# The feed-forward part's hidden values: bias from ScalarE to VectorE, rounding from GpSimd to ScalarE

## The chip, the cores and the metric

The kernel runs on one core of a Trainium2 chip. The metric is the device time of one execution in microseconds. The core's engines that matter here: TensorE (PE, matrix products; its weight loads are listed as PEld), VectorE (DVE), ScalarE (ACT), GpSimd (POOL) and SyncE (SP), whose queue issues the DMAs. Each takes its own instructions in the order in which the program gives them; they wait for one another by semaphores.

## The reference

The input is 32 images of 56 x 56 pixels with 96 channels. Layer 0 is a convolution block with weights mixed per image: 1x1 expansion to 384 channels, 3x3 depthwise convolution, 1x1 projection, each with batch normalization, and the input added. Layer 1 treats the 3136 pixels of an image as tokens: a layer normalization, a token mixer that goes through a Fourier transform and back, an addition, and then the feed-forward part that the change concerns:

```
t = t + _L1_ffn_ref(_ln_t(t), W1, b1, W2, b2)

q_mul = lambda x: _float_quantize(x, 5, 2)     # 8 bits: 5 of exponent, 2 of mantissa
q_acc = lambda x: _float_quantize(x, 5, 10)    # 16 bits: float16

def _qlinear(x, W, b):
    y = q_acc(jnp.einsum('bsk,nk->bsn', q_mul(x), q_mul(W)))
    return q_acc(y + q_mul(b))
h = jax.nn.relu(_qlinear(x, W1, b1))           # 96 -> 384
y = _qlinear(h, W2, b2)                        # 384 -> 96; rounds h to 8 bits first
```

So a hidden value is a sum rounded to float16, plus a bias, rounded to float16 again, cut at zero, and rounded to 8 bits before the second product.

## The kernel before

Images are independent, and the kernel keeps several of them in flight: the convolution of one runs beside the Fourier and feed-forward steps of earlier ones. `record(b)` (line 767) lists the operations of image b. An image has two halves h for the convolution, 3 chunks c of 128 hidden channels for each, and 4 strips `st` of 784 pixels (`T`) for the token steps.

- Convolution. `by_tensor` (line 928) computes a chunk with PE, with DMAs that regroup the pixels before it (hp<-h) and after it (h<-hp). `by_vector` (line 869) computes a chunk with VectorE: PE expands, ScalarE moves the values to SBUF and makes a first pass over each half of the tile (ACT h<-h,small), VectorE adds the eight other taps (DVE h<-h,small,h 128x784, in place), ScalarE cuts at zero.
- Token mixer. Layer-norm moments (`ln`) with bn_stats on VectorE and the root on GpSimd, products `ha` and `g`, then seven groups of frequencies (`za`, `zb`, `tmpa`, `tmpb`, `zo`, `y`), in which ScalarE and VectorE alternate, then the way back.
- Feed-forward part (the loop `for st in range(NS)`), once a strip: the mixer's result is added (`xs`), moments and normalization (`nt`, 8 bits), a turn back on PE (`n8`), and then for each of the 3 chunks of hidden channels, from line 1412 on:
  - PE: two products of 392 columns into two banks of PSUM (`up`);
  - ScalarE: a copy from PSUM to `h16`, float16;
  - ScalarE: in place, bias and Relu (from line 1429);
  - GpSimd: a copy that rounds `h16` to `h8`, 8 bits (from line 1434);
  - later PE: the second product (`down`), which reads the three `h8` tiles.
  That is 12 such tiles an image and 384 in all. `h16` has 2 buffers, `h8` has 6 (lines 735 and 736). After `down`, ScalarE copies to `y16`, VectorE adds a bias to it in float16 (DVE TENSOR_SCALAR y<-y,fb 96x784, the only operation of this kind in the image loop), GpSimd adds it to `xs`, and a DMA writes the result.

What runs in which order is written by a planner. `Plan.add` (line 219 on) takes for each operation an engine, an assumed duration, a due time and the buffers that it reads and writes. To each due time a number out of a fixed list is added by the operation's place in the list. `Plan.order` (line 269) simulates the engines with the assumed durations and returns the operations in the order of their simulated starts; `for op in plan.order(): op.emit()` (line 1478) issues them. `Pinned` (line 370) keeps each engine's instructions in that order. The planner only names the engine of an operation; which engine executes it is decided by the function that is passed to be emitted. So two operations that the planner starts one after the other reach the program one after the other, whichever engine they go to. All pinned instructions bear line 380, which is why the profile tells them apart by tile names and shapes.

The helper that gives each engine's instructions its waits works from the tiles: an instruction waits for the last one that wrote what it reads, and for the last ones that read what it overwrites.

Of the kernel before, what the change touches and what calls it, by code (L numbers as in the profile page):

```python
# [14 lines left out]
AF = mybir.ActivationFunctionType  # L15
ALU = mybir.AluOpType
# [202 lines left out]
class Plan:  # L219
# [16 lines left out]
    def add(self, eng, dur, due, emit, reads=(), writes=(), takes=(), size=0, port=None, slack=0.0):  # L236
        op = Op()
        op.seq = len(self.ops)
        due += NUDGE[op.seq % len(NUDGE)]
        if eng in ("DVE", "ACT") and any(isinstance(k[0], Buf) and isinstance(k[0].ring, Banks) for k in reads):  # L240
            due -= HURRY
        op.eng, op.dur, op.due, op.emit = eng, dur, round(due, 3), emit
        op.takes, op.size, op.slack = list(takes), size, slack
        op.port = eng == "POOL" if port is None else port
        op.after, op.ready, op.end = [], 0.0, None
        before = set()
        for key in reads:
            if key in self.writer:
                before.add(self.writer[key])
        for key in writes:  # L250
            if key in self.writer:
                before.add(self.writer[key])
            before.update(self.readers.get(key, ()))
        for key in writes:
            self.writer[key] = op
            self.readers[key] = []
        for key in reads:
            if key not in writes:
                self.readers.setdefault(key, []).append(op)
        op.left = len(before)  # L260
        for b in sorted(before, key=lambda o: o.seq):
            b.after.append(op)
        op.bufs = list(dict.fromkeys(key[0] for key in (*reads, *writes) if isinstance(key[0], Buf)))
        for b in op.bufs:
            b.users += 1
        self.ops.append(op)
        return op
# [118 lines left out]
def kernel(  # L386
# [26 lines left out]
    def const(shape, dt, name):  # L413
        return cp.tile(shape, dt, tag=name, name=name)
# [62 lines left out]
    fb1 = const([128, NC3], F32, "fb1")  # L477
# [261 lines left out]
    for r in (r_in, r_xs, r_da, r_dd, r_g2, r_yt):  # L739
# [6 lines left out]
    te, ve, se, po, sy = (  # L746
        Pinned(tc, e) for e in (nc.tensor, nc.vector, nc.scalar, nc.gpsimd, nc.sync)
    )
# [3 lines left out]
    def cols(engine, n):  # L752
        return {"DVE": n / 960 + 0.125, "ACT": n / 1200 + 0.05}[engine]

    def halves(ap):
        return ap.rearrange("p (j t) -> p j t", j=2)
# [10 lines left out]
    def record(b):  # L767
# [572 lines left out]
        for st in range(NS):  # L1340
# [56 lines left out]
            def turn_back(ps=ps, nt=nt):  # L1397
                for q in range(SQ):
# [9 lines left out]
                    saturate=False,  # L1408
                ),
                reads=[(ps, 0)], writes=[(n8, 0)],  # L1410
            )
            h8s = []
            for c in range(NC3):
                ps, h16, h8 = Buf(banks, 2), Buf(r_h16), Buf(r_h8)

                def up(c=c, ps=ps, n8=n8):
                    for j in range(2):
                        te.matmul(
                            ps.pair[:, 512 * j : 512 * j + TH], fw1[:, 128 * c : 128 * c + 128],
                            n8.ap[:, j * TH : j * TH + TH], start=True, stop=True,  # L1420
                        )

                add("PE", 0.36, due + 7, up, reads=[(n8, 0)], writes=[(ps, 0)], takes=[ps, h16])
                add(
                    "ACT", cols("ACT", T), due + 8,
                    lambda ps=ps, h16=h16: se.copy(halves(h16.ap), halves(ps.pair)[:, :, 0:TH]),
                    reads=[(ps, 0)], writes=[(h16, 0)],
                )
                add(
                    "ACT", 0.86, due + 9,  # L1430
                    lambda c=c, h16=h16: se.activation(h16.ap, h16.ap, AF.Relu, bias=fb1[:, c : c + 1]),
                    writes=[(h16, 0)],
                )
                add(
                    "POOL", 0.82, due + 9.5,
                    lambda h16=h16, h8=h8: po.tensor_copy(h8.ap, h16.ap, saturate=False),
                    reads=[(h16, 0)], writes=[(h8, 0)], takes=[h8],
                )
                h8s.append(h8)
# [35 lines left out]
    for b in range(NB):  # L1475
        record(b)
# [115 lines left out]
```

## Time and profile before

| what | value |
|---|---|
| three timed runs | 4315.35, 4319.36, 4329.76 us (median 4319.36) |
| profiled execution, time | 4307.71 us |
| profiled execution, span from first to last instruction | 4305.9 us |
| granted TensorE clock, mean | 0.967 |
| VectorE, busy | 3661.1 us, 9036 instructions |
| ScalarE, busy | 3092.0 us, 6281 instructions |
| GpSimd, busy | 1627.6 us, 1332 instructions |
| copy to h16 on ScalarE (ACT CAST h<-ps 128x784) | x384, mean 815 ns |
| ScalarE, rounding of the normalized values (ACT n<-ps 96x784 fp8e5) | x128, mean 827 ns |
| ScalarE, Relu without bias (ACT h<-h 128x784 f32) | x192, mean 858 ns |
| taps on VectorE (DVE h<-h,small,h 128x784) | x1536, mean 1063 ns |

How to read it: a group's line gives the engine, the operation, the tile written and those read, the shapes, the number of such instructions, then their busy time in us and the mean of one in ns, and after the bar the idle time of the engine just before them with what ended it. A timeline's line gives start, duration, and the instruction; "x3" merges three in a row, and consecutive instructions of VectorE and ScalarE overlap a little in it, so that durations add up to slightly more than the time from start to start. The chain of waits goes back from the last instruction, at each step to what released it, and gives shares of the span.

In the middle of the run the same pattern of instructions returns with every image: the period of the h tiles is 126.6 us from 1360.0 to 1486.6 and 126.0 us from 1486.6 to 1612.6.

### The profile page before, as it was taken

What the parts mean: (1) busy time and instruction counts of PE and PEld (TensorE: products, weight loads), DVE (VectorE), ACT (ScalarE), POOL (GpSimd) and SP (SyncE); (2) the same over time, 40 slices, a digit from 0 to 9 for tenths busy, and PEclk for the clock granted to TensorE, in tenths of its full rate; (3) what the DMA queues carried; (4) which work ended last, traced back from release to release, by engine and by line L of the source; (5) the groups of instructions that cost most, each with busy time, mean ns of one, the idle gap of its engine ahead of it and who ended that gap; (6) DMA issues with size and microseconds to landing.
All of it is one profiled execution on the core that took longest, in us unless ns stands there. A gap on an engine that the chain in (4) does not pass through costs nothing.

```text
span 4305.9 us, 104378 instructions
## 1 busy us (share of the span) xinstructions
PE 3833.1 (89%) x40066; PEld 2422.4 (56%) x40066; DVE 3661.1 (85%) x9036; ACT 3092.0 (72%) x6281; POOL 1627.6 (38%) x1332
## 2 busy tenths in 40 slices
PE   2899999899999998899999999998999999999985
PEld 0466565555565555555556556555565555556564
DVE  5898988888998888988898898887988888998762
ACT  1467777677787776777777787776777777787665
POOL 1224333443333443433443434343433443434333
PEclk9999999999999999999999999999999999999995
DMA  4776667676667766667677667766667776667651
GB/s 118 142 166 150 158 170 173 148 170 158 154 172 180 170 162 157 152 154 174 155 175 169 151 159 175 175 158 152 151 155 178 163 171 159 153 160 171 148 143 58
DMA packets 427749, 679.25 MB, mean 158 GB/s; under 512 B 155062, under 2 KB 290678, under 8 KB 427206
## 3 DMA queue, kind: packets, MB, share of 16 engines
q1 hardware_dynamic: 421632, 668.08, 66.3%
q8 instruction: 316, 5.18, 0.6%
q10 hardware_dynamic: 5618, 4.49, 0.4%
q14 instruction: 183, 1.50, 0.1%
HBM read 300.21 MB, written 211.04 MB: 119 GB/s over the span
## 4 chain that ended last, share of the span: by engine, by line
DVE 36%; PE 28%; ACT 22%; issue 6%; DMA 5%; POOL 1%; SPq 0%; POOLq 0%; ACTq 0%; DVEq 0%
PE ps L380 28%; DVE h L380 8%; ACT h L380 8%; DVE ln L380 6%; ACT nt L380 4%; DVE ha L380 3%; DVE za L380 3%; DVE tmpa L380 3%; DVE tmpb L380 3%; DMA hp<-h 3%; DVE zb L380 3%; DVE wk L380 2%; ACT tmpa L380 2%; ACT g L380 1%; DVE wkc L380 1%
## 5 line engine op out<-in xcount | busy, mean ns | idle before, releaser
L380 DVE SCALAR_TENSOR_TENSOR h<-h,small,h 128x784 f32<-128x784 f32 x1536 | 1569.5, 1063 | 61.0 <-ACT h L380 54.8
L380 POOL CAST h<-h 128x784 fp8e5<-128x784 f16 x384 | 604.2, 1578 | 1397.9 <-ACT h L380 1397.8
L380 PE MATMUL ps<-x,wk 97*32 97x435 f32 (+2 forms) x3840 | 686.7, 569 | 21.0 <-DVE wk L380 17.3
L380 PE MATMUL ps<-dftb_s,g 112*64 112x112 f32 (+1 forms) x3776 | 420.3, 281 | 31.4 <-DVE ln L380 16.6
L380 ACT ACTIVATE h<-ps 128x435 f32<-128x435 f32 (+2 forms) x768 | 389.7, 546 | 67.9 <-PE ps L380 66.8
L380 DVE SCALAR_TENSOR_TENSOR ha<-ps,ln,nshift 120x192 f32<-120x192 f32 x896 | 306.0, 407 | 154.7 <-PE ps L380 153.7
L380 POOL TENSOR_TENSOR ln<-ln,mhalf 120x7 f32<-120x7 f32 (+1 forms) x256 | 429.2, 1676 | 21.3
L380 PE MATMUL ps<-hp,wg 32*32 32x392 f32 x12288 | 390.0, 523 | 27.8 <-issue 20.9
L380 PEld LDWEIGHTS ps<-dftb_s,g 112*64 112x64 f32 (+1 forms) x3776 | 341.0, 168 | 128.6 <-issue 40.9
L380 DVE BATCH_NORM_STATS2 ln<-ps 112x6 f32<-112x96 f32 (+1 forms) x1792 | 318.1, 248 | 86.5 <-PE ps L380 83.1
L380 PEld LDWEIGHTS ps<-x,wk 97*32 97x32 f32 (+1 forms) x3840 | 206.9, 125 | 297.1 <-issue 191.1
L380 ACT ACTIVATE hp<-ps,small 128x392 f32<-128x392 f32 x384 | 212.3, 591 | 225.0 <-PE ps L380 183.3
L380 ACT ACTIVATE h<-h,fb 128x784 f16<-128x784 f16 x384 | 366.4, 965 | 0.3
L380 ACT ACTIVATE nt<-ps,ln 112x96 fp8e5<-112x96 f32 x896 | 302.5, 437 | 75.0 <-DVE ln L380 74.9
L380 ACT ACTIVATE h<-h 128x784 f32<-128x784 f32 x192 | 164.4, 858 | 264.5 <-DVE h L380 264.5
L380 PE MATMUL ps<-w1c,x 96*120 96x192 f32 x1792 | 340.1, 337 | 6.6 <-issue 6.6
L380 POOL TENSOR_TENSOR xs<-xs,y 96x784 f32<-96x784 f32 x128 | 237.2, 1854 | 251.5 <-DVE y L380 164.4
L380 PEld LDWEIGHTS <-fw 96*128 96x128 fp8e5 (+1 forms) x1536 | 155.1, 114 | 284.8 <-issue 209.6
L380 PEld LDWEIGHTS ps<-w1c,x 96*120 96x120 f32 x1792 | 296.9, 188 | 32.7 <-issue 28.3
L380 ACT CAST h<-ps 128x784 f16<-128x784 f32 x384 | 302.5, 815 | 17.5 <-PE ps L380 16.1
L380 PEld LDWEIGHTS ps<-hp,wg 32*32 32x32 f32 x12288 | 221.4, 106 | 166.5 <-issue 83.3
L380 PE MATMUL ps<-h,wkc 128*96 128x392 f32 x768 | 284.9, 519 | 0.0
(171 smaller groups left out, 7180.0 us busy)
## 6 DMA issues: line engine op xcount, KB each, us to landing
hp<-h SPq DMA_DIRECT2D x384, 217.5 KB
h<-hp SPq DMA_DIRECT2D x384, 196.0 KB
gd<-g SPq DMA_DIRECT2D x384, 192.0 KB
g<-gd SPq DMA_DIRECT2D x192, 336.0 KB
dd<-ddd SPq DMA_DIRECT2D x128, 392.0 KB
yt<-yd SPq DMA_DIRECT2D x128, 336.0 KB
xd<-park SPq DMA_DIRECT2D x128, 294.0 KB
xs<-xd SPq DMA_DIRECT2D x128, 294.0 KB
```

The costliest lines, as they stand in the source:

```text
L380: return self.tc.keep_in_program_order(method(*args, **kwargs))
```

## The change

The bias and the Relu of h go to VectorE: one tensor_scalar with two operations, addition of the per-partition bias and maximum with zero, float16 in place. The rounding to 8 bits goes from GpSimd to ScalarE, as an activation Copy. The engine names, durations and due times that are handed to the planner stay as they were ("ACT" and "POOL"), so that the simulated schedule and the order in which all operations are issued are the same: VectorE meets a bias at the place in the order where ScalarE had it, and ScalarE meets a rounding where GpSimd had it.

```diff
                 add(
                     "ACT", 0.86, due + 9,
-                    lambda c=c, h16=h16: se.activation(h16.ap, h16.ap, AF.Relu, bias=fb1[:, c : c + 1]),
+                    lambda c=c, h16=h16: ve.tensor_scalar(
+                        h16.ap, h16.ap, fb1[:, c : c + 1], 0.0, ALU.add, ALU.max
+                    ),
                     writes=[(h16, 0)],
                 )
                 add(
                     "POOL", 0.82, due + 9.5,
-                    lambda h16=h16, h8=h8: po.tensor_copy(h8.ap, h16.ap, saturate=False),
+                    lambda h16=h16, h8=h8: se.activation(h8.ap, h16.ap, AF.Copy, saturate=False),
                     reads=[(h16, 0)], writes=[(h8, 0)], takes=[h8],
                 )
```

## Prediction

> **What bounds the kernel now.** I read the busy times first, then the chain of work that ended last, then one image's time on each engine (1486.6 to 1612.6 us), then the groups of the three operations concerned.
>
> ```profile
> PE 3833.1 (89%) x40066; PEld 2422.4 (56%) x40066; DVE 3661.1 (85%) x9036; ACT 3092.0 (72%) x6281; POOL 1627.6 (38%) x1332
> ```
>
> ```profile
> DVE 36%; PE 28%; ACT 22%; issue 6%; DMA 5%; POOL 1%; SPq 0%; POOLq 0%; ACTq 0%; DVEq 0%
> ```
>
> Three engines share the chain, so an average says little. The timeline of VectorE over one image sorts it out (columns: start us, us, then the instruction; the last bracket is idle time before it).
>
> ```profile
> 1497.56 0.91 DVE L380 SCALAR_TENSOR_TENSOR tmpb<-zb,tmpb 128x112 f32<-128x112 f32 x1
> ...
> 1520.66 2.38 DVE L380 SCALAR_TENSOR_TENSOR wk<-wpw_s,mix,wk 97x384 f32<-97x384 f32 x3
> 1522.96 0.26 DVE L380 SCALAR_TENSOR_TENSOR zb<-tmpb,zb 128x112 f32<-128x112 f32 x1
> 1523.15 0.90 DVE L380 TENSOR_TENSOR ln<-ln 120x7 f32<-120x7 f32 x2
> ...
> 1543.43 14.85 DVE L380 SCALAR_TENSOR_TENSOR h<-h,small,h 128x784 f32<-128x784 f32 x15
> ...
> 1562.43 1.25 DVE L380 BATCH_NORM_STATS2 ln<-ps 120x6 f32<-120x96 f32 x7 [1.97 <-PE ps L380]
> ```
>
> From 1579.4 to the next image's 1543.5 (about 90 us of 126) VectorE idles 2.1 us in all: this phase is its own. From 1546.4 to 1577.7 PE runs with two short gaps and VectorE waits for it: PE's phase. GpSimd at the same moments:
>
> ```profile
> 1497.31 1.03 POOL L380 CAST h<-h 128x784 fp8e5<-128x784 f16 x1 [7.35 <-ACT h L380]
> ...
> 1521.58 1.05 POOL L380 CAST h<-h 128x784 fp8e5<-128x784 f16 x1 [10.88 <-ACT h L380]
> 1522.80 1.15 POOL L380 CAST h<-h 128x784 fp8e5<-128x784 f16 x1 [0.17 <-ACT h L380]
> ```
>
> The tmpb operation that takes 0.91 us under the first cast takes 0.27 at 1502.23, with no cast; the two ln operations that take 0.90 under the third take 0.24 at 1500.29. So a cast stops VectorE. ScalarE around the last two casts:
>
> ```profile
> 1520.55 0.97 ACT L380 ACTIVATE h<-h,fb 128x784 f16<-128x784 f16 x1
> 1521.40 0.48 ACT L380 COPY zo<-ps 112x384 f32<-112x384 f32 x1
> 1521.76 0.97 ACT L380 ACTIVATE h<-h,fb 128x784 f16<-128x784 f16 x1
> 1522.61 0.60 ACT L380 ACTIVATE tmpa<-ps,fa 128x280 f32<-128x280 f32 x1
> ```
>
> And the groups (busy us, mean ns of one, idle before):
>
> ```profile
> L380 POOL CAST h<-h 128x784 fp8e5<-128x784 f16 x384 | 604.2, 1578 | 1397.9 <-ACT h L380 1397.8
> ...
> L380 ACT ACTIVATE h<-h,fb 128x784 f16<-128x784 f16 x384 | 366.4, 965 | 0.3
> ...
> L380 DVE TENSOR_SCALAR y<-y,fb 96x784 f16<-96x784 f16 x128 | 54.4, 425 | 52.5 <-ACT y L380 49.7
> ```
>
> **What the Trainium skill says.** "SBUF — State Buffer", section "Who interferes with whom": GpSimd and a VectorE operation with two SBUF inputs, or in a two-port mode, exclude each other; the loser blocks for the whole instruction. The trace agrees (0.91 against 0.27 us above). "VectorE: DVE Perf Modes", section "The perf-mode tier table": tensor_scalar on 16-bit SBUF data reaches the fourfold mode; the y row, same length and form, has 402 ns at least and 411 in the median. "ScalarE: Activation LUTs", section "What ACT_TABLE_LOAD costs": an ACTIVATE with immediates is 186 ns + 0.833 ns an element, and a pointer operand adds some 93 ns: estimates 839 and 932 ns for 784 elements; the trace has 858 (the Relu without bias) and 965.
>
> **The change, part by part.** An image has 12 h tiles (384 in all). Starts are counted, since neighbours overlap by about 0.08 us.
>
> *Removed from ScalarE:* 12 bias+Relu, 0.85 us each start to start (1520.55 to 1521.40). *Added there:* 12 roundings. No row has f16 to fp8 on ScalarE; between the n row (fp8 from PSUM, 827 ns) and the 858 Relu I take 0.83, start to start 0.75. Its own sum is a gain of 1.2 us an image, in 72% busy, so worth nothing by itself.
>
> *Added on VectorE:* 12 tensor_scalar, 0.33 us start to start, as y's (1505.17 to 1505.50). That form has one operation and this one two; bounds 0.33 and, at half the rate, 0.33+784/4/960 = 0.53. I take 0.33, since y shows the mode and the rest is alike. It is 3.96 us an image.
>
> *Removed from GpSimd:* 12 casts. GpSimd does not bound, but what they blocked comes back to VectorE. Start to start against the same operations unblocked: tmpa pair 1486.68 (1.25 for 0.60) 0.65; za pair 0.64; tmpb 0.65; wk 2.30 for 1.92, 0.38; ln pair 0.66; ln triple at 1594.40 (0.90 for 0.25) 0.65. Sum 3.63 us, plus some 0.4 on taps. Over all VectorE rows that overlap a cast, time above the unblocked median is 130 us, or 4.06 an image. So 3.96 in, 4.06 out: balanced. Behind the casts GpSimd has the park copy, the wg products and the layer-norm root. They start up to 1 us earlier; each still meets one VectorE operation, so I put that at zero, with 0.3 us an image either way as its bound. No DMA and nothing on SP's queue moves.
>
> *The new waits.* VectorE's bias waits for ScalarE's copy: in the steady images the copy ended 0.2 to 3 us before VectorE comes to that turn, so it stops nobody. ScalarE's rounding waits for VectorE, and behind it queue the evictions of PSUM. By the turns of the changed program, nine of an image's twelve fall in VectorE's phase; I walk them with the running shift of VectorE:
> - 0 to 2 (1588 to 1595): +0.99-0.65 = +0.34. ScalarE stands some 0.5, 0.6 and 1.1 us for the biases, and its first pass over the next tap tile ends at 1597.7 instead of 1595.8. The tap that needs it comes at 1597.47+0.34: just in time, and ScalarE's wait of 1.80 us at 1597.58 is the cover. If 0.1 us of cover is gone, VectorE pays.
> - 3 and 4 (1485.9 to 1489): +0.66-1.29, shift -0.29. The second rounding fills a gap of 0.99 before zo.
> - 5 (1496.8): +0.33-0.65, shift -0.61.
> - 6 and 7: wk ends at 1521.97, bias until 1522.38, rounding, then tmpa at 1523.19 and until 1523.79. VectorE is at its za (1524.30 before) at 1523.31, and waits 0.50. Shift -0.61-0.38+0.66-0.66+0.50 = -0.49.
> - 8: +0.33: shift -0.16 where the image hands over to PE.
> - 9 to 11 lie in PE's phase: +0.66 against 1.4 us between VectorE's last x update (1560.46) and the PE transposes that read it (1561.90). Covered.
>
> So 31 images x -0.16 = -5 us. In the tail (after 4150) VectorE idles and the chain runs through copies, Relus and casts: a tile's bias costs 0.41+0.06 in place of 0.97, saving about 0.5 us on some 14 tiles, -7; against it one bias waits from 4244.9 to 4250.3 and holds the residual addition (4247.89) behind it for 2.8 us. Tail -4. Total -9 against the profiled execution (span 4305.9, time 4307.7, 12 below the median of 4319.4). The forecast is put on the median: 4310.
>
> **Rivals.**
> - *The hand-over costs (slower).* The place is ScalarE in turns 0 to 2 and 6: it stands for a bias that VectorE does late, and evictions behind it come 0.9 to 1.9 us late. For: two of my steps have margins near 0.1 us. Against: ScalarE idles 28%. It decides once ScalarE's lateness at a tap tile's first pass is over 0.1 us; if 1.3 of the 1.9 us passes on, 31 x 1.3 = 40 in place of the -5: with the tail's -4, 4355.
> - *The freed port pays in full (faster).* If turn 6 doesn't wait, and the taps' 0.4 counts: -0.16-0.50-0.4 = -1.06 an image, -33, with the tail 4282. For: the chain view has 85 of the 130 blocked us on it, and only 204 of the 384 bias places (67 us). Against: the wk operations precede bias 6 in every image.
> - *The bias runs at half rate:* 9 x 0.20 x 31 = 56 on top of the forecast, 4366. Against: y.
> - That the change isn't made is excluded: the changed program has 384 more instructions on VectorE, 384 fewer on GpSimd, and as many as before on ScalarE.
>
> **How the numbers follow.** About 0.3% (13 us) is what a measurement of this kernel can tell from no change: 4306.4 to 4332.3. Balance 50%, its own range 4294 to 4330 (0.4 us an image either way, and the tail's gain): of that 17 faster, 29 same, 4 slower. Hand-over 27%, slower. Freed port 19%, faster. Half rate 4%, slower. So faster 0.36, same 0.29, slower 0.35. The range, 4280 to 4354, leaves out the half rate, the dearer part of the hand-over and the better end of the freed port, some 2 in 10.
>
> **What would show it.** VectorE's new row at 0.41 us x384 and its busy time within 20 us of 3661; ScalarE's rounding near 0.83; the tmpb, za and ln groups at their unblocked means; ScalarE's waits for VectorE up by some 4 us an image, and VectorE's for tmpa by 0.5. I am wrong if the bias row is over 0.45 us, if other GpSimd work takes the casts' place in blocking VectorE, or if VectorE waits for ScalarE at the taps.

## The result and the profile after

| kernel | median of the runs | ratio to before, 95% interval |
|---|---|---|
| before, 7 runs | 4319.36 us | |
| changed, 7 runs (4343.98 to 4371.79) | 4350.05 us | 1.008 (1.0056 to 1.0103) |

The change makes the kernel 31 us slower, where 9 us less were forecast; 4350 is near the upper end of the stated range (4280 to 4354), on the other side of before. The profiled execution took 4343.98 us, span 4342.2 (before 4305.9), mean granted TensorE clock 0.961 (before 0.967). Busy times and the chain that ended last, from the page of the changed kernel:

```profile
PE 3858.6 (89%) x40066; PEld 2508.2 (58%) x40066; DVE 3670.9 (85%) x9420; ACT 3085.8 (71%) x6281; POOL 1059.9 (24%) x948
```

```profile
PE 37%; DVE 30%; ACT 23%; issue 4%; DMA 3%; POOL 0%; SPq 0%; DVEq 0%; POOLq 0%; ACTq 0%
```

VectorE has 384 instructions more and is busy only 9.8 us longer: the balance of added biases and freed port came out. But its share of the chain fell from 36 to 30% and PE's rose from 28 to 37%. The two new groups (busy us, mean ns of one, idle before):

```profile
L380 ACT ACTIVATE h<-h 128x784 fp8e5<-128x784 f16 x384 | 328.4, 856 | 160.3 <-DVE h L380 157.0
L380 DVE TENSOR_SCALAR h<-h,fb 128x784 f16<-128x784 f16 x384 | 158.2, 419 | 28.0 <-ACT h L380 28.0
```

Both durations are near the forecast's (0.83 and 0.41). New is what stands before the rounding: ScalarE idles 157 us for VectorE's biases. The list of waits says the same (waiting engine and tile, then whom for; us in total, times, longest):

```profile
ACT h L380 <- DVE h L380: 362.1, 338, 4.2
...
PE ps L380 <- ACT y L380: 92.4, 57, 2.2
...
DVE za L380 <- ACT za L380: 73.5, 59, 2.2
```

Before, these were 264.5, 45.1 and 21.2 us. All three meet in turns 6 to 8 of the hidden tiles: in the 29 images counted below, 76 of the 160 us that ScalarE idles before roundings lie there, 60 of the 92 of PE, and 23 of the 74 of VectorE (43 of these lie in turns 3 to 5). The timeline of the changed kernel there (start, us, instruction; idle before in brackets):

```profile
1153.61 0.75 DVE L380 TENSOR_SCALAR h<-h,fb 128x784 f16<-128x784 f16 x2
...
1154.06 0.86 ACT L380 ACTIVATE h<-h 128x784 fp8e5<-128x784 f16 x1 [1.66 <-DVE h L380]
...
1155.90 0.51 DVE L380 SCALAR_TENSOR_TENSOR za<-ps,fa,tmpa 128x280 f32<-128x280 f32 x1 [0.86 <-ACT za L380]
...
1156.84 0.85 ACT L380 ACTIVATE h<-h 128x784 fp8e5<-128x784 f16 x1
...
1158.02 0.48 ACT L380 COPY y<-ps 112x384 f32<-112x384 f32 x1
1158.04 2.30 POOL L380 TENSOR_TENSOR wg<-mask,small 128x512 f32<-128x512 f32 x2 [1.12 <-DVE small L380]
...
1158.55 0.49 PE L380 MATMUL ps<-n,fw 96*128 96x392 fp8e5 x2 [2.24 <-ACT y L380]
...
1159.33 1.83 DVE L380 SCALAR_TENSOR_TENSOR h<-h,small,h 128x784 f32<-128x784 f32 x1
```

and the same matmuls, the tap, the wg products and rounding 8 before:

```profile
1148.56 0.49 PE L380 MATMUL ps<-n,fw 96*128 96x392 fp8e5 x2 [0.54 <-ACT y L380]
...
1148.80 1.07 POOL L380 TENSOR_TENSOR wg<-mask,small 128x512 f32<-128x512 f32 x1
...
1150.09 1.03 DVE L380 SCALAR_TENSOR_TENSOR h<-h,small,h 128x784 f32<-128x784 f32 x1
...
1151.20 0.97 POOL L380 CAST h<-h 128x784 fp8e5<-128x784 f16 x1 [1.34 <-ACT h L380]
...
1152.14 1.06 POOL L380 TENSOR_TENSOR wg<-mask,small 128x512 f32<-128x512 f32 x1
1152.34 2.35 DVE L380 SCALAR_TENSOR_TENSOR ha<-ps,ln,nshift 120x192 f32<-120x192 f32 x7
```

Three things are to be seen. ScalarE stands 1.66 us for the bias of turn 6 and then rounds, so that its copy of za is late and VectorE waits 0.86. Roundings 6 and 7 put off the y copy behind them, and PE pauses 2.24 us for it, not 0.54. And GpSimd runs two wg products in a row ("x2", 2.30 us) where rounding 8 used to stand between them: the tap under the second takes 1.83 us, not 1.02 (medians of 27 images, the same as in these lines within 0.01).

**Where the time went.** I cut both profiled executions at the same VectorE instructions (biases of h not counted) in the 29 images from the third to the thirty-first, and sorted the pieces by the granted TensorE clock. The clock's records know two levels, 1.0 and 0.5; "half" below is a piece in which the mean is under 0.985. Median length in us, number of pieces in brackets:

| stretch | before, full | before, half | after, full | after, half |
|---|---|---|---|---|
| turns 6 to 8 (28 instructions from the first wk) | 13.09 (29) | none | 14.73 (13) | 15.58 (16) |
| PE's phase, instructions 62 to 88 | 21.97 (19) | 27.57 (10) | 21.94 (23) | 25.08 (6) |
| PE's phase, 88 to 132 | 15.44 (24) | 19.40 (5) | 15.44 (27) | 19.18 (2) |
| turns 3 to 5 (166 to 200) | 16.78 (22) | 18.54 (7) | 16.36 (21) | 18.71 (8) |

Summed over the 29 images, turns 6 to 8 lose 59 us: 1.64 in each image but the first two, and some 14 for the half clock in 16 of them. Turns 0 to 2 (instructions 132 to 146) lose 29 x 0.34 = 10. Turns 3 to 5 give back 5 and PE's phases 39, these only because fewer of their pieces have half clock (8, not 15), and for a shorter time: their length at full clock is unchanged. With 11 us in the rest of the run that makes the 36 between the two spans.

### The profile page after: what moved, and what is told of

It is laid out like the page before. It is cut to its first block, busy times and chain, and to the rows that moved or that the text cites. A ratio compares the mean times of both kernels' runs of the same rounds, so it can differ in the third digit from the quotient of the medians.

```text
span 4342.2 us, 104145 instructions
## 1 busy us (share of the span) xinstructions
PE 3858.6 (89%) x40066; PEld 2508.2 (58%) x40066; DVE 3670.9 (85%) x9420; ACT 3085.8 (71%) x6281; POOL 1059.9 (24%) x948
## 4 chain that ended last, share of the span: by engine, by line
PE 37%; DVE 30%; ACT 23%; issue 4%; DMA 3%; POOL 0%; SPq 0%; DVEq 0%; POOLq 0%; ACTq 0%
PE ps L380 37%; DVE h L380 10%; ACT h L380 8%; DVE ln L380 6%; ACT nt L380 4%; DVE za L380 3%; DVE tmpb L380 2%; DVE ha L380 2%; ACT tmpa L380 2%; DVE wk L380 2%; DVE tmpa L380 2%; ACT tmpb L380 2%; DVE zb L380 2%; ACT y L380 1%; ACT hp L380 1%
## 5 line engine op out<-in xcount | busy, mean ns | idle before, releaser
L380 ACT ACTIVATE h<-h 128x784 f32<-128x784 f32 (+1 forms) x576 | 489.9, 857 | 365.4 <-DVE h L380 362.1
L380 POOL TENSOR_SCALAR ln<-ln 120x7 f32<-120x7 f32 (+1 forms) x256 | 84.0, 328 | 1427.5 <-DVE ln L380 1427.3
L380 PE MATMUL ps<-hp,wg 32*32 32x392 f32 x12288 | 377.9, 517 | 12.7 <-DMA hp<-h 5.9
L380 PE MATMUL ps<-w1c,x 96*120 96x192 f32 x1792 | 359.3, 351 | 4.6 <-issue 4.6
L380 PEld LDWEIGHTS ps<-w1c,x 96*120 96x120 f32 x1792 | 318.4, 199 | 31.3 <-issue 25.7
L380 POOL COPY park<-x 96x784 f32<-96x784 f32 x128 | 112.4, 878 | 856.2 <-DVE x L380 615.6
L380 PE MATMUL ps<-n,fw 96*128 96x392 fp8e5 x768 | 198.9, 351 | 123.4 <-ACT y L380 62.7
## 6 DMA issues: line engine op xcount, KB each, us to landing
h<-hp SPq DMA_DIRECT2D x384, 196.0 KB
```

Of the source, the lines that this page charges most:

```text
L380: return self.tc.keep_in_program_order(method(*args, **kwargs))
```

## The experiments

Before ran beside them on the same chips, with medians of 4317.77 (first four), 4322.09 (next four) and 4319.04 us (last four). Theory 1 was that ScalarE's hand-over at turns 4 and 6 is the price; theory 2, the rival, that VectorE's added instruction is, freed port or not; theory 3, that the freed GpSimd blocks a tap.

| run | us, median | ratio to before, 95% interval |
|---|---|---|
| e1_bias_only | 4439.14 | 1.029 (1.0265 to 1.0315) |
| e2_cast_only | 4377.19 | 1.0135 (1.011 to 1.0161) |
| e3_wg_held | 4342.67 | 1.0059 (1.0039 to 1.0079) |
| e4_late6 | 4309.63 | 0.9978 (0.9966 to 0.9991) |
| e5_late4 | 4353.82 | 1.0078 (1.0057 to 1.01) |
| e6_late46 | 4312.99 | 0.9982 (0.9971 to 0.9993) |
| e7_late46_wg | 4294.97 | 0.9937 (0.9912 to 0.9961) |
| e8_replan | 4953.27 | 1.1475 (1.1447 to 1.1502) |
| e9_late6_wg | 4293.33 | 0.9938 (0.9922 to 0.9953) |
| e10_pool4 | 4338.18 | 1.004 (1.0028 to 1.0052) |
| e11_late6_wg_pool4 | 4279.65 | 0.9904 (0.989 to 0.9918) |
| e12_pause | 4335.41 | 1.0037 (1.0023 to 1.0051) |

### Each half alone: e1 and e2

In the changed kernel, for e1:

```diff
-                    lambda h16=h16, h8=h8: se.activation(h8.ap, h16.ap, AF.Copy, saturate=False),
+                    lambda h16=h16, h8=h8: po.tensor_copy(h8.ap, h16.ap, saturate=False),
```

> The first half of the change alone: bias and lower bound on VectorE, the rounding left on GpSimd. Theory 1 (ScalarE's hand-over at turns 4 and 6 is the price of the change): ScalarE no longer stands for the bias and the rounding never lies in its queue, so this costs VectorE's own term only, at most 12 x 0.33 = 3.96 us an image, less what was idle before (turns 9 to 11, 2 or 3 of the 12 in the matmul stage): below 4319 + 31 x 3.96 = 4442, and as likely 4319 + 31 x 2 = 4380. Theory 2 (VectorE's added instruction is the price, whatever frees the port): 31 x 2.97 = 92 us above before, 4411, and the wait of ScalarE for the rounding plays no part. Theory 3 (freed GpSimd runs the second wg product against a tap): nothing of it here, since the casts still stand in GpSimd's queue.

The kernel before, for e2:

```diff
-                    lambda h16=h16, h8=h8: po.tensor_copy(h8.ap, h16.ap, saturate=False),
+                    lambda h16=h16, h8=h8: se.activation(h8.ap, h16.ap, AF.Copy, saturate=False),
```

> The second half alone: the rounding on ScalarE directly behind its own bias, nothing added to VectorE. Theory 1 (hand-over): no wait of ScalarE on VectorE between bias and rounding is left, ScalarE only carries 12 x 0.75 = 9 us an image more; VectorE gets the 4.06 us an image of freed taps back less what ScalarE's lateness eats: 4194 (4319 - 31 x 4.06) to 4300. Theory 2 (VectorE's added bias is the price): 4319 - 31 x 4.06 + 31 x 0.81 (wg product) = about 4219. If it is ScalarE's time itself and no wait that is short, 4350 or more. Theory 3 alone says: the second wg product starts right behind the first here too, and the tap beside it takes 1.8 us in place of 1.0.

Both halves alone are slower than the whole: +121 and +59 us, together 180, against 31 for both. Each pays for the other. In e1 VectorE is busy 3801.9 us, 140.8 more than before, and the time follows nearly in full; at 0.367 us a bias this is the forecast's 12 x 0.33 an image, and a little more. An image of e1 that is at full clock throughout takes 129.97 us (5 images; before 126.08, 16 images), and 31 x 3.89 = 121. So VectorE's own term is the price of this half. 4439 is at the upper bound of theory 1 (4442) and 28 above the figure of theory 2 (4411); both take this term, and e1 doesn't decide between them. In e2 VectorE is busy 3525.5 us, 135.6 less than before (the forecast had put the freed port at 130), and yet the kernel is slower, because ScalarE carries bias and rounding, 3372.8 us busy, and VectorE waits for it. Groups of e2:

```profile
L380 DVE SCALAR_TENSOR_TENSOR za<-ps,fa,tmpa 128x224 f32<-128x224 f32 x192 | 86.0, 448 | 148.6 <-ACT tmpa L380 81.5 <-ACT za L380 67.1
L380 DVE SCALAR_TENSOR_TENSOR za<-ps,fa,tmpa 128x280 f32<-128x280 f32 x32 | 16.3, 509 | 34.0 <-ACT za L380 33.3 <-ACT tmpa L380 0.6
```

Before, the idle times of these two were 58.7 and 0.7 us. Here no rounding waits for VectorE: it is ScalarE's own time that comes short, which e2's expectation had as its third case (4350 or more); the figures of theories 1 and 2 (4300 at most, and 4219) both miss. Theory 3's sign is there: the tap takes 1.83 us, where before and e1, whose casts stand between the wg products, have 1.02.

### Turn 6: e4

The operations are issued in the planner's order; the rounding of turn 6 is held back until two further instructions of ScalarE are out, or until an operation that uses its buffers comes. (`st` and `c` count tiles as the program lists them. In the planner's order tile (2, 1) comes ahead of (2, 0): it is turn 6.)

```diff
+                if (st, c) == (2, 1):
+                    late[cast] = 2
...
+        if op in late:
+            held.append([late[op], op])
+            continue
...
         op.emit()
+        if op.eng == "ACT" and op not in biases:
+            for h in held:
+                h[0] -= 1
+        while held and held[0][0] <= 0:
+            held.pop(0)[1].emit()
```

> The changed kernel with the rounding of turn 6 put two ScalarE instructions later in ScalarE's queue, so that ScalarE does not stand for VectorE's bias before the copies that VectorE waits for; nothing else differs. Theory 1: the wait of VectorE for za ahead of its 280 wide sum (0.86 us) goes from turn 6, 31 x 0.9 = 28 us less than the changed kernel, about 4322. Theories 2 and 3: no change, 4350 (within 8).

4309.63, 40 us less than the changed kernel, and 0.22% below before. In its timeline the two copies run first, VectorE's sum has no wait, and PE's pause is 1.29 us:

```profile
1155.55 0.85 ACT L380 ACTIVATE h<-h 128x784 fp8e5<-128x784 f16 x1
...
1156.44 0.51 DVE L380 SCALAR_TENSOR_TENSOR za<-ps,fa,tmpa 128x280 f32<-128x280 f32 x1
...
1159.09 0.49 PE L380 MATMUL ps<-n,fw 96*128 96x392 fp8e5 x2 [1.29 <-ACT y L380]
```

The stretch is 13.79 us long at full clock (14.73 in the changed kernel), and half clock is there in 1 piece of 29 and no longer in 16. 29 x 0.94 = 27 and 15 x 0.85 = 13 come to the 40 between the medians; the 28 expected left the half clock out. So the place of one instruction on ScalarE decides the sign of the change: theory 1 holds at turn 6. (The two profiled executions differ by 19 us only. They are e4's slowest, with half clock in 15 pieces of turns 3 to 5, and the changed kernel's fastest, with 8.)

### The wg product: e3, and later e7 and e9

```diff
-                    lambda h16=h16, h8=h8: se.activation(h8.ap, h16.ap, AF.Copy, saturate=False),
+                    lambda h16=h16, h8=h8, st=st, c=c: (
+                        se.activation(h8.ap, h16.ap, AF.Copy, saturate=False),
+                        po.tensor_copy(spare, h8.ap[:, 0:1]) if (st, c) == (2, 2) else None,
+                    ),
```

> The changed kernel with GpSimd's second wg product held until rounding 8 has ended, by a copy of one column on GpSimd that reads the rounded tile, as the casts held it before. Theory 3 (0.81 us an image of the loss is the tap that the second wg product blocks): the tap is back at 1.0 us, 31 x 0.81 = 25 us less than the changed kernel, about 4325. Theories 1 and 2: no change, 4350 (within 8).

4342.67: 7 us less than the changed kernel, inside the uncertainty of either and well short of 25. The tap did come back: the stretch at full clock went from 14.73 to 13.92. In the pieces with half clock, though, the tap's 0.81 us gives next to nothing: those with 3.41 us of half clock take 14.91 us (changed 14.96), those with 6.83 us 16.20 (16.26). So the tap pays in the images at full clock alone, 11 of the last 27: 11 x 0.81 = 9. Over all 29 turns 6 to 8 take 11 us less (429.4 and 440.4). The 25 expected counted every image. In a kernel in which rounding 6 is late too, few of these pieces have half clock, and the same edit is worth more. e7 is e6 (below) with it, e9 is e4 with it:

> Both roundings later and the second wg product held behind rounding 8. Theory 3 (the tap that the wg product blocks lies on the path): 25 us less than with both roundings later, about 4250 to 4270. If the 0.8 us that the tap gives back is absorbed before the image ends, as the 7 us of the held product alone suggest: within 8 of the version with both roundings later.

> The changed kernel with the rounding of turn 6 two ScalarE instructions later and the second wg product held behind rounding 8; the rounding of turn 4 where the change put it. If the two terms of turns 6 to 8 add and the place of rounding 4 is worth nothing: the same as with all three, 4295 (within 8), 55 less than the changed kernel. If the later rounding 4 had helped after all: 4305 to 4315.

e7 is 18 us below e6, e9 is 16 below e4; the intervals of each pair do not overlap. e9 came out as expected. e7 missed both its figures: 25 less than e6 would be 4288, where 4250 to 4270 was written. The timeline of e9:

```profile
1151.66 1.06 POOL L380 TENSOR_TENSOR wg<-mask,small 128x512 f32<-128x512 f32 x1
...
1152.95 1.02 DVE L380 SCALAR_TENSOR_TENSOR h<-h,small,h 128x784 f32<-128x784 f32 x1
...
1155.41 1.07 POOL L380 TENSOR_TENSOR wg<-mask,small 128x512 f32<-128x512 f32 x1
1155.54 2.35 DVE L380 SCALAR_TENSOR_TENSOR ha<-ps,ln,nshift 120x192 f32<-120x192 f32 x7
```

One wg product, then the tap in 1.02 us, then the other. Its turns 6 to 8 last 12.98 us at full clock, against 13.09 before and 13.79 in e4. Theory 3 stands, at 16 to 18 us in place of 25.

### Turn 4: e5, e6 and e10

e5 and e6 use the edit of e4: `late[cast] = 5` for tile (1, 1), turn 4, in e5, this and turn 6 in e6.

> The changed kernel with the rounding of turn 4 alone put five ScalarE instructions later, behind the za copy that VectorE's 224 wide sum waits for (0.90 us in the image shown, 1.0 to 1.2 us later than before in the median image). Theory 1 (hand-over at turns 4 and 6): 31 x 0.5 to 31 x 1.2 off the changed kernel's 4350, 4313 to 4335; below 4350 in any case. Theory 2 (VectorE's added instruction is the price everywhere): no change, 4350 (within 8). A third way: the rounding of turn 4 now ends just ahead of the matmuls that read it and delays them by up to 0.9 us, so that the gain is given back: 4350 or above.

> Both roundings later, that of turn 4 by five ScalarE instructions and that of turn 6 by two. Theory 1: the two waits stand in different stretches of the image and add, so the gain of late6 (4310) and that of turn 4 alone (15 to 37 us) add to 4273 to 4295. If VectorE only moves its wait to the next buffer or to TensorE, no better than 4305.

No gain: 4353.82 (changed 4350.05), and 4312.99 (e4 4309.63). Theory 1 falls at turn 4. The timeline of e5 shows why:

```profile
1257.06 0.45 DVE L380 SCALAR_TENSOR_TENSOR za<-ps,fa,tmpa 128x224 f32<-128x224 f32 x1 [0.29 <-ACT za L380]
...
1260.16 0.33 DVE L380 SCALAR_TENSOR_TENSOR zb<-ps,fb,tmpb 128x112 f32<-128x112 f32 x1 [1.16 <-ACT tmpb L380]
```

In the changed kernel the same two wait 0.90 and 0.41 us. The wait moved to a later sum: in the images at full clock, median, -0.75 us at za and +0.74 at zb. Perhaps the rounding's 0.86 us on ScalarE is itself too much here. e10 gives only this rounding back to GpSimd:

```diff
+                        po.tensor_copy(h8.ap, h16.ap, saturate=False)
+                        if (st, c) == (1, 1)
+                        else se.activation(h8.ap, h16.ap, AF.Copy, saturate=False)
```

> The changed kernel with the rounding of turn 4 alone given back to GpSimd. If in turns 3 to 5 it is ScalarE's 0.86 us itself that is short and not the rounding's place: VectorE's wait for za and zb goes (about 1 us an image), less the 0.34 us that a rounding on GpSimd takes from VectorE's taps (4.06 us by 12): 31 x 0.4 to 31 x 0.7, 12 to 20 less than the changed kernel, 4330 to 4338. If VectorE then waits for something else there: 4350 to 4362.

> The version with rounding 6 later and the wg product held, and rounding 4 on GpSimd besides. If the terms add: 12 to 20 below that version, 4275 to 4283. If the rounding on GpSimd costs what it frees: within 8 of it, 4287 to 4303.

4338.18 and 4279.65, 12 and 14 us less than the same kernels without the edit, as expected. Over the median image VectorE loses 0.59 and 0.41 us on the two operations that the rounding now blocks and gains 1.34 on the wait for za; turns 3 to 5 last 15.91 us at full clock (16.36 in the changed kernel, 16.78 before). So in turns 3 to 5 ScalarE's time is what is short, in both places in the order that were tried. e11 is the fastest: 1% below before.

### The pause of TensorE: e12

The kernel of e7 with two copies of a constant on ScalarE ahead of the y copy of turn 7:

```diff
+            for _ in range(2):
+                se.copy(spare2, wpw_s[:, 0, 0:192])
```

> The version with both roundings later and the wg product held (4295), with two small copies of a constant on ScalarE ahead of the y copy of turn 7, so that TensorE's pause for it grows from 1.29 us to about 1.9 in each image while VectorE's queue is left as it was; the copies feed nothing. If a long pause of TensorE is what brings the half clock into turns 6 to 8 (0 of 29 images at a pause of 0.54, 5 of 56 at 1.3, 80 of 144 at 1.8 to 2.2 in the runs so far): half clock in about 15 of 29 images, and 15 x 0.85 = 13 us more with up to 0.3 an image for the later h copy, 4305 to 4320. If the pause has nothing to do with it (the wait of VectorE, or the time of the image, does it): 4 of 29 images as before, 4295 to 4305.

4335.41, 40 us more than e7: the direction as expected, but above the stated range, which was 10 to 25 more. (The counts of images from all traces are in the last section; those of the expectation leave e6 out.) The timeline of e12:

```profile
1166.27 0.73 ACT L380 CAST spare<-wpw_s 97x192 f16<-97x192 f32 x2
...
1167.43 0.49 PE L380 MATMUL ps<-n,fw 96*128 96x392 fp8e5 x2 [1.93 <-ACT y L380]
```

Half clock came into turns 6 to 8 in 13 of 29 images (4 in e7). Such a stretch took 14.66 us against 13.27 with full clock, and the full one itself was 0.29 longer than e7's (12.98), since the later h copy puts off VectorE's bias of turn 8. Over the 29 images the stretch takes 25 us more than in e7 (408.7 and 383.3). The other 15 us are not told apart.

### A new plan: e8

The bias labelled "DVE" with 0.333 us and as a user of the port that GpSimd shares, the rounding "ACT" with 0.75:

```diff
-                    "ACT", 0.86, due + 9,
+                    "DVE", 0.333, due + 9,
...
+                    port=True, writes=[(h16, 0)],
...
-                    "POOL", 0.82, due + 9.5,
+                    "ACT", 0.75, due + 9.5,
```

> The changed kernel with the order of turns made anew: the planner is told that the bias is VectorE's (0.333 us, using the port that GpSimd shares) and the rounding ScalarE's (0.75 us), where the changed kernel kept the order made for bias on ScalarE and rounding on GpSimd. Theory 1 (roundings in places that the planner never chose for ScalarE): the planner gives ScalarE's copies for VectorE the place that they had, so 4280 to 4320. Theory 2 (VectorE's added instruction): 4350 whatever the order. A planner whose order suits its own model and not the chip may give anything to 4400.

4953.27, out of all bounds. PE, VectorE and ScalarE are busy 85, 76 and 62% of the span (89, 85 and 71 in the changed kernel): the true labels give another order of everything, and that order leaves all three engines idle for longer. It tells nothing of the hand-over. That the planner's list of due-time offsets was fitted to the old labels would explain it; this was not tried.

## Why the prediction was wrong, point by point

- **Prices: right.** The bias at 419 ns a piece (forecast 0.41) and the rounding at 856 (0.83). What the Trainium skill's "VectorE: DVE Perf Modes", "The perf-mode tier table", says of tensor_scalar thus holds with two operations (0.33 us start to start in the median) as with the one of y, and the rival of the half rate falls.
- **"3.96 in, 4.06 out: balanced": right.** e1 put the bias at 140.8 us of VectorE's busy time, e2 the freed port at 135.6, and the changed kernel is 9.8 above before.
- **Turns 0 to 2, +0.34: right.** Measured +0.34 (instructions 132 to 146). The rival put the hand-over's danger here and at turn 6; here it cost nothing.
- **"Waits 0.50" at turn 6: right place and mechanism, wrong size.** VectorE waited 0.86 us, and e4 took 0.94 us an image away. I had counted the late copy of tmpa; VectorE's sum needs the za copy as well, which stands behind tmpa on ScalarE (1154.82 and 1155.29).
- **"I put that at zero" for GpSimd's work behind the casts: the step that failed most.** The forecast said that each still meets one VectorE operation. The second wg product stood behind the cast of turn 8 and ran beside the ha operations, which read PSUM and take 2.35 us for seven (in e9 too, where it runs beside them again): it cost nothing, which fits the Trainium skill's "SBUF — State Buffer", "Who interferes with whom": a VectorE operation with at most one SBUF input, outside the two-port modes, does not contend with GpSimd. Now it meets a tap, which has two: 1.83 for 1.02 us, 0.81 an image against my bound of 0.3. e7 and e9 measure 16 to 18 us for it.
- **Turns 3 to 5: -0.95 forecast, -0.42 measured at full clock.** "The second rounding fills a gap of 0.99 before zo" took for free room what ScalarE needed for the copies after it: VectorE's wait for za there, in the median image, is 1.44 us and was 0.38. e5 shows that five ScalarE instructions later is no better, e10 that it is the 0.86 us itself.
- **"Turns 6 to 8" as a whole: +0.45 forecast, +1.64 measured**, of which 0.81 is the tap and 0.38 the rest of the wait at za.
- **Sum.** -0.16 + 0.36 + 0.02 (rounding) + 0.81 + 0.53 = +1.56 an image at full clock, in place of -0.16: 48 us over 31 images. With the half clock below, 62; PE's phases give 39 back.
- **Not in the forecast: the clock.** I followed VectorE alone, and took no account of what roundings 6 and 7 do to the y copy behind them and so to PE. The pause of 2.24 us goes with half clock in 16 of 29 images, 14 us. Nor did I expect PE's phases to get 39 us shorter.
- **Tail, -4 forecast: wrong.** From the start of VectorE's last tap to the end it is 196.0 us (192.7 before), at a clock of 0.712 (0.721). I did not try which of the two terms failed.

In size the rival "the hand-over costs" came nearest (4355), with part of its reason: turn 6, not turns 0 to 2, and a third party, GpSimd. That its figure is so near is luck: nothing in it stood for the 39 us that PE's phases gave back.

Why they did stays open, but it is not the lot of one execution. The pieces of PE's phases with half clock are 15 in the profiled executions of before and of e1, which have all roundings on GpSimd, and 5 to 11 in those of the other eleven (e8, with its own plan, left out), which have all or all but one on ScalarE. The two phases together take 1158 and 1166 us in the former and 1113 to 1125 in the latter. Longer turns 6 to 8 don't explain it: e11, with 12.98 us and no half clock there, has 10 such pieces in PE's phases, and e10, with 14.73 us and half clock in 25 images, has 9. No run here changes only the three roundings that lie in PE's phase.

## What to carry to other kernels

Work that leaves an engine frees whatever queued behind it: ask when that work will now start, and against which instruction of another engine, before its price is put at zero. Work that enters an in-order queue is priced by every copy behind it, for each engine that reads one of them, not by the sum of busy times; moving the one instruction (here two places, 40 us) can be worth more than the change. A pause that it causes on a third engine belongs in the price too. And where two halves of a change are slower by themselves, that says nothing of the whole: +121 and +59 made +31, and with three places mended -39.

## What the runs showed of the hardware that was not expected

- A longer pause of TensorE makes half clock around its end likelier. The longest pause of PE in turns 6 to 8 and the images with half clock there, the first two counted images left out since their pause is another: 0.54 us, 0 of 27 (before); 1.3 us, 9 of 135 (e4, e6, e7, e9, e11); 1.8 to 1.9 us, 44 of 81 (e1, e2, e12); 2.2 us, 73 of 108 (changed, e3, e5, e10). In these 126 images the half clock sets in between 0.8 us before the end of the pause and 1.6 us after it, and lasts 3.41 or 6.83 us. e12 made the pause longer by ScalarE's copies and got it in 13 images in place of 4. The length of the stretch is not the reason: at full clock e12's is shorter (13.27 us) than e4's (13.79), which has half clock in 1 of 27. All this is from one execution of each kernel. Windows of 14 us from the first wk operation, before and then changed (busy us and count of PE, PEld, DVE, ACT, POOL, then the clock):

```profile
1394.40:1408.40 14.00, 12.79 (x92) 8.51 (x91) 13.64 (x32) 9.95 (x19) 7.19 (x8) 1.00 0.16 53
```

```profile
1406.30:1420.30 14.00, 11.68 (x61) 9.10 (x61) 12.45 (x29) 7.36 (x13) 4.00 (x4) 0.76 0.17 52
```

  In the second, the matmuls after the pause take longer:

```profile
1413.71 0.81 PE L380 MATMUL ps<-n,fw 96*128 96x392 fp8e5 x2 [2.24 <-ACT y L380]
1414.31 1.51 PE L380 MATMUL ps<-h,fw 128*96 128x392 fp8e5 x4
```

  The first pair had 0.49 us in the image shown above, where the clock stayed at 1.0 in spite of the same pause: a chance, and no run here shows what decides it.
- What a rounding takes on GpSimd depends on its place. Before, the median by place in the image goes from 0.84 to 5.88 us (the mean of all is 1.58). The rounding of turn 4 takes 0.91 us before and 1.96 in e10, where it is the only one there, and VectorE's operations beside it are longer by the 0.59 and 0.41 us above.
